# Third cycle of the rotations: the couplings of two blocks in one product of two columns, and the last pair turned and added between the products of its second layer

## The chip, the cores and the metric

The kernel runs on one core of a Trainium2 chip. The metric is the device time of one execution in microseconds, given as the median of several runs. The engines are TensorE (PE in the profile, with PEld for its weight loads), VectorE (DVE), ScalarE (ACT), GpSimd (POOL) and SyncE (SP), which here only issues DMAs.

## The reference

A small hybrid network on `x` of 2 x 2048 tokens x 256 features, all in fp32. Two attentions alternate with two uses of the same feed-forward part:

```python
x = x + attn_a(layernorm(x))
x = x + ffn(layernorm(x))
x = x + attn_b(layernorm(x))
x = x + ffn(layernorm(x))

def ffn(x):
    gf = global_net(x.mean(axis=1))                # one value a batch
    out = x
    for _ in range(3):                             # three cycles
        h = gelu(out @ w1 + b1)                    # 256 -> 256
        h = gelu(h @ w2 + b2)                      # 256 -> 128
        h = gelu(h @ w3 + b3)                      # 128 -> 64
        tf = sigmoid(h @ w4 + b4)                  # 64 -> 1, one value a token
        coupling = 0.1 + adaptive_range * (0.7 * gf + 0.3 * tf - 0.5) * 2.0
        o_r, o_i, p_r, p_i = split(out, 4)
        out = out + coupling * concat(p_r, -p_i, -o_r, o_i)
    return out
```

The change is in the third cycle of `ffn` and in the addition of its result to `x`.

## The kernel before

**Tiling.** The 4096 tokens are cut into 8 blocks of 512 (`BLK`). The normalized input of a feed-forward part lies feature-major in `zq` (128 partitions x 2 halves of the features x 4096 tokens), the residual stream `x` token-major in `xs` (128 tokens x 32 tiles x 256 features). All of this stays in on-chip memory; `x` is written out by the last feed-forward part.

**The rotations.** `rotations(n, part, store)` makes the steps of feed-forward part n (0 between the attentions, 1 at the end, where `store` is true). A step k = 0 to 11 stands for one pair of blocks, 2 * (k % 4) and the next, in cycle k // 4; so k = 8 to 11 are the third cycle. For each k:

- `first(k, e)` (L789) takes block e of the pair through w1: two halves m of the 256 outputs, each a product (L796) into its own PSUM bank and a Gelu on ACT (L797).
- `second(k)` (L800): w2 for both blocks, L806, Gelu L808.
- `third(k)` (L811): w3 for both blocks (L816). The 64 outputs of block 0 stand in rows 0 to 63 of one bank, those of block 1 in rows 64 to 127, so that one Gelu (L818) makes one tile `a3` of 128 rows for the pair.
- `fourth(k)` (L821): the couplings, and the block turned. In the first two cycles the coupling is made for all rows at once and `z` is changed in place (L829 to L841). In the third cycle it goes to `back` (L843).

**`back`.** The result of the third cycle is wanted token-major, to be added to `xs`. So the couplings are made by token: for each block e of the pair, four products (L851), one for each 128 tokens, of 64 rows of `a3` and the column `w4`, each giving 128 tokens x 1. In fp32 each product shows as two records in the profile, so 16 for a pair. Then a tanh of 128 x 4 on ACT (L856), the coupling from it on DVE (L857) and its negative (L858). After both blocks' couplings come the halves: for each block e and each half h of its tokens, TensorE turns 2 x 2 squares of `z` into one bank `trf` (L870), DVE adds it to `xs` in two operations of 128 x 256 (L874), then adds the twisted quarters times the coupling in four operations of 128 x 128 (L882, `scalar_tensor_tensor`), and, in the second feed-forward part, SP issues a DMA of 256 KB (L888) that stores the half.

**The order.** The program order on each engine is the one in which the steps are called; nothing reorders it afterwards. In the steady part `rounds(f, n)` (L1173) calls for even n `fourth(k - 2)`, `second(k - 1)`, `first(k, 0)` and for odd n `third(k - 1)`, `first(k, 1)`, with k = n // 2. The end of the first feed-forward part is written out by hand, with the steps of attention b's first blocks, `zero` and `one`, between:

```python
        zero.norm(work)
        first(11, 0)
        third(10)
        one.look()
        first(11, 1)
        one.norm(late)
        fourth(10)
        second(11)
        zero.turn()
        third(11)
```

after which come `zero.query()`, `zero.rotate()`, `zero.key()` and `fourth(11, zero.rotate)` (the latter calls a second `rotate` between the two blocks of the pair). The second feed-forward part ends with `for n in range(8, 27): rounds(f, n)`: its last calls are `fourth(9)`, `second(10)`, `first(11, 0)`, `third(10)`, `first(11, 1)`, `fourth(10)`, `second(11)`, `third(11)`, `fourth(11)`.

**Buffers.** `bank()` gives the next of seven PSUM banks in turn, so an operation of TensorE that opens a bank waits until the one that had it seven banks ago has been read. `take("small", ...)` gives the next of eight buffers in a ring, `hold.tile` a place for good.

**Names in the profile.** `q1f`, `q2f`, `q3f`, `q4f` are the banks of the four layers, `trf` those of the transposes; `a1f`, `a2f`, `a3f` the Gelus' results; `cf` the couplings. `pv`, `rotk`, `swapks` belong to attention b; `p1f` and `gmf` to the global net (`context`, L767), `L945` to attention b's projections.

Of the kernel before, what the change touches and what calls it, by code (L numbers as in the profile page):

```python
# [9 lines left out]
F32 = mybir.dt.float32  # L10
F32R = mybir.dt.float32r
AF = mybir.ActivationFunctionType
ALU = mybir.AluOpType
# [3 lines left out]
P = 128  # L17
B, N, D = 2, 2048, 256
# [3 lines left out]
BPB = N // BLK  # L22
# [45 lines left out]
def tile_hybrid(ctx: ExitStack, tc: tile.TileContext, x: bass.AP, consts: bass.AP, wa_d: bass.AP, wf_d: bass.AP, wb_d: bass.AP, out: bass.AP):  # L68
    nc = tc.nc
    mm = nc.tensor.matmul  # L70

    keep = ctx.enter_context(tc.tile_pool(name="keep", bufs=1))
    small = keep.tile([P, _CONST["cols"][0]], F32, name="small")
# [4 lines left out]
    zq = keep.tile([P, 2, T], F32, name="zq")  # L78
# [6 lines left out]
    def const(name):  # L85
        return small[:, _CONST[name][0] : _CONST[name][1]]

    def view(t, at, name, rows=P):
        return t[:rows, at[name][0] : at[name][1]]

    ident, mean_w, ones = const("ident"), const("mean"), const("ones")
    sign = const("sign")

    def blk(t, j):
        return t[:, :, j * BLK : (j + 1) * BLK]

    def tokens(j):
        return xs[:, 4 * j : 4 * j + 4, :]
# [37 lines left out]
    def in_order(first, which=(engines.PE, engines.DVE, engines.Activation, engines.Pool)):  # L136

        last = {}
        for ins in nc.cur_bb.bb.instructions[first:]:
            if ins.engine in which:  # L140
                if ins.engine in last:
                    tc.add_manual_dep(
                        ins, last[ins.engine].name,
                        mybir.DependencyInfo(mybir.DependencyClass.NoSync, mybir.DependencyReason.DATA),
                        reason="order of the program",
                    )
                last[ins.engine] = ins
# [563 lines left out]
    def behind(tail):  # L711
        wf, wb = weights["wf"], weights["wb"]
        late = later_pools["late"]
        hold = ctx.enter_context(tc.tile_pool(name="hold", bufs=1, reuse_waits="tile"))
# [8 lines left out]
        def take(tag, shape, name):  # L723
            if tag == "kt2":
                return work.tile(shape, F32, tag="kt", name=name)
            if tag in ("og", "kt", "swap"):
                return own.tile(shape, F32, tag=tag, name=name, bufs=2 if tag == "swap" else 1)
            return work.tile(shape, F32, tag=tag, name=name, bufs=rings.get(tag, 1))

        def bank(name):  # L730
            return ps.tile([P, BLK], F32, tag="ps", name=name)
# [6 lines left out]
        w4, b3 = view(wf, _WF, "w4"), view(wf, _WF, "b3")  # L738
# [5 lines left out]
        hb4 = hold.tile([P, 1], F32, name="f_hb4")  # L744
# [4 lines left out]
        plain = hold.tile([P, 1], F32, name="f_plain")  # L749
        nc.vector.tensor_scalar(plain, view(wf, _WF, "range"), 0.3, None, ALU.mult)  # L750
        beta = hold.tile([P, 1], F32, name="f_beta")
        nc.vector.tensor_scalar(beta, plain, sign, None, ALU.mult)

        def rotations(n, part, store):
            alphas, plains = {}, {}
            acts, narrow = {}, {}

            def context(b):

# [26 lines left out]
            def blocks(k):  # L786
                return 2 * (k % 4), 2 * (k % 4) + 1

            def first(k, e):  # L789

                z = blk(zq, blocks(k)[e])
                a1 = take((("qs", "ks"), ("rotq", "rotk"))[k % 2][e], [P, 2, BLK], f"a1f{n}_{k}_{e}")
                for m in range(2):
                    q1 = bank(f"q1f{n}_{k}_{e}_{m}")
                    for c in range(2):
                        mm(q1, w1[:, c, m * P : (m + 1) * P], z[:, c, :], start=(c == 0), stop=(c == 1))  # L796
                    nc.scalar.activation(a1[:, m, :], q1, AF.Gelu, bias=b1[:, m : m + 1])  # L797
                acts[k, e] = a1

            def second(k):  # L800
                narrow[k] = []
                for e in range(2):
                    a1 = acts.pop((k, e))
                    q2 = bank(f"q2f{n}_{k}_{e}")
                    for c in range(2):
                        mm(q2, w2[:, c, :], a1[:, c, :], start=(c == 0), stop=(c == 1))  # L806
                    a2 = take("en", [P, BLK], f"a2f{n}_{k}_{e}")
                    nc.scalar.activation(a2, q2, AF.Gelu, bias=b2)  # L808
                    narrow[k].append(a2)

            def third(k):  # L811

# [8 lines left out]
            def fourth(k, between=None):  # L821
# [8 lines left out]
                for e in range(2):  # L830
# [9 lines left out]
                    nc.vector.tensor_tensor(z[:, 0, :], z[:, 0, :], t0, ALU.add)  # L840
                    nc.gpsimd.tensor_tensor(z[:, 1, :], z[:, 1, :], t1, ALU.subtract)  # L841

            def back(k, js, a3, between):  # L843


                both = []
                for e in range(2):
                    row = slice(64 * e, 64 * e + 64)
                    q4 = bank(f"q4f{n}_{k}_{e}")
                    for tile in range(4):  # L850
                        mm(  # L851
                            q4[:, tile : tile + 1], a3[row, tile * P : (tile + 1) * P], w4[row, 0:1],
                            start=True, stop=True,
                        )
                    tt = take("small", [P, 3, 4], f"cf{n}_{k}_{e}")
                    nc.scalar.activation(tt[:, 2, :], q4[:, 0:4], AF.Tanh, bias=hb4, scale=0.5)  # L856
                    nc.vector.tensor_scalar(tt[:, 0, :], tt[:, 2, :], plain, plains[js[e] // BPB], ALU.mult, ALU.add)  # L857
                    nc.vector.tensor_scalar(tt[:, 1, :], tt[:, 0, :], -1.0, None, ALU.mult)  # L858
                    both.append(tt)
                for e in range(2):  # L860
                    j, cs, z = js[e], both[e], blk(zq, js[e])
                    if e == 1 and between:
                        between()
                    for h in range(2):
                        tr = bank(f"trf{n}_{k}_{e}_{h}")
                        for q in range(2):
                            at = slice((2 * h + q) * P, (2 * h + q + 1) * P)
                            for c in range(2):
                                to = q * D + (1 - c) * P
                                nc.tensor.transpose(tr[:, to : to + P], z[:, c, at], ident)  # L870
                        tr = tr.rearrange("p (q s f) -> p q s f", q=2, s=2)
                        half = tokens(j)[:, 2 * h : 2 * h + 2, :].rearrange("p q (s f) -> p q s f", s=2)
                        for s in range(2):
                            nc.vector.tensor_tensor(half[:, :, s, :], half[:, :, s, :], tr[:, :, 1 - s, :], ALU.add)  # L874
                        for q in range(2):
                            tile = 2 * h + q

                            x4, t4 = (
                                a.rearrange("p s (u f) -> p (s u) f", u=2) for a in (half[:, q, :, :], tr[:, q, :, :])
                            )  # L880
                            for m, quarters in enumerate((slice(0, 4, 3), slice(1, 3))):
                                nc.vector.scalar_tensor_tensor(  # L882
                                    x4[:, quarters, :], t4[:, quarters, :], cs[:, m, tile : tile + 1],
                                    x4[:, quarters, :], ALU.mult, ALU.add,
                                )
                        if store:
                            s0 = (j % BPB) * BLK + 2 * h * P
                            nc.sync.dma_start(  # L888
                                out[j // BPB, s0 : s0 + 2 * P, :].rearrange("(t p) d -> p t d", p=P),
                                tokens(j)[:, 2 * h : 2 * h + 2, :],  # L890
                            )

            return context, first, second, third, fourth


        sums1 = hold.tile([P, 2, NB], F32, name="sums1")
# [273 lines left out]
        blocks = [Block(j) for j in range(NB)]  # L1170
        tail = tail(bank)

        def rounds(f, n):  # L1173

            context, first, second, third, fourth = f
            k = n // 2
            if n % 2 == 0:
                if 0 <= k - 2:
                    fourth(k - 2)
                if 0 <= k - 1 < 12:  # L1180
                    second(k - 1)
                if k < 12:
                    first(k, 0)
            else:
                if 0 <= k - 1:
                    third(k - 1)
                if k < 12:
                    first(k, 1)

        f = rotations(0, sums0, False)  # L1190
        context, first, second, third, fourth = f
        turned, looked = first_norms, {}

        def block_of(j):
# [91 lines left out]
        one.turn()  # L1286

        f = rotations(1, sums1, True)
        context, first, second, third, fourth = f
        front, front1 = context(0), context(1)  # L1290
        for j, x in enumerate(blocks):
            before = blocks[j - 1] if j else None
# [76 lines left out]
        third(2)  # L1369
        first(3, 1)  # L1370
        next(front1)
        for n in range(8, 27):
            rounds(f, n)
        in_order(begin)

    behind(attention_a())
# [117 lines left out]
```

## Time and profile before

| | us |
|---|---|
| median of 3 runs | 2184.47 (2184.06 to 2188.18) |
| the profiled execution | 2182.7 |
| its span | 2180.8 |
| TensorE busy in it | 2136.0 |
| mean granted TensorE clock | 0.993 |
| one step k of the second feed-forward part in its steady rounds | 14.86 |
| last scaled add (L882) ends | 2177.73 |

Times of single events are counted from the start of the span. The clock is given as a share of full speed. Attention a takes the first 1,560 us or so; the third cycle of the first feed-forward part begins about 1696 and runs into attention b at 1733 to 1757; the second feed-forward part's third cycle ends with the program. In a row of a timeline, the columns are start, duration, engine, line, operation, result and operands, shape and count; in the chain of waits, start and duration of a piece of work that the end waited for.

### The profile page before, as it was taken

To read this page: it belongs to the slowest core of one execution; us is meant where nothing else is said; L and a number is where in the kernel's file an instruction comes from. 1 tells how busy PE (TensorE), PEld (TensorE's weight loads), DVE (VectorE), ACT (ScalarE), POOL (GpSimd) and SP (SyncE) were. 2 spreads that over 40 slices of the span, in tenths; PEclk is the share of its full clock that TensorE was granted. 3 is DMA by queue.
4 is the path that set the end of the run, shared out by engine and by line. 5 is a ranking of instruction groups with operands and counts; after the bars stand their busy time and mean duration, and the time that the engine had idled before them with its cause. 6 is when DMAs were issued, how large, how long until landed. Compare 5 with 4: busy or idle time off the path is not lost.

```text
span 2180.8 us, 38972 instructions
## 1 busy us (share of the span) xinstructions
PE 2136.0 (98%) x14346; PEld 1028.5 (47%) x14346; DVE 1725.7 (79%) x3319; ACT 1434.0 (66%) x2780; POOL 348.6 (16%) x318
## 2 busy tenths in 40 slices
PE   8899999999999999999999999999999999999998
PEld 3344444444444444444444444444444567676434
DVE  6789998998999899899899899987144688886435
ACT  3367777777776777777677777777864445554442
POOL 3100000000001000000000000000145345541450
PEclk9999999999999999999999999999999999999999
DMA  6410110101101011010110101100100000000002
GB/s 184 135 58 14 41 36 16 46 12 45 36 16 45 10 48 36 16 39 17 48 35 17 36 19 48 36 16 7 51 1 1 1 1 2 1 2 1 1 0 78
DMA packets 53552, 68.21 MB, mean 31 GB/s; under 512 B 18800, under 2 KB 27888, under 8 KB 53104
## 3 DMA queue, kind: packets, MB, share of 16 engines
q1 hardware_dynamic: 52448, 64.26, 10.6%
q8 instruction: 113, 1.85, 0.3%
q10 hardware_dynamic: 720, 0.92, 0.1%
q14 instruction: 79, 0.65, 0.1%
q0 software_dynamic: 192, 0.52, 0.1%
HBM read 35.26 MB, written 25.69 MB: 28 GB/s over the span
## 4 chain that ended last, share of the span: by engine, by line
PE 86%; DVE 8%; DMA 2%; ACT 1%; SPq 1%; issue 1%; POOL 1%; DVEq 0%; ACTq 0%; POOLq 0%
PE av L620 21%; PE s L378 19%; PE p L633 10%; PE q1f L796 7%; PE p L637 7%; DVE mx L382 5%; PE q2f L806 4%; PE pe L1084 2%; PE po L487 2%; PE bpo L1110 1%; PE pv L954 1%; PE pw L954 1%; PE pq L945 1%; PE q3f L816 1%; PE pk L945 1%; DMA xs<-in_x 1%
## 5 line engine op out<-in xcount | busy, mean ns | idle before, releaser
L382 DVE TENSOR_REDUCE mx<-s 128x1 f32<-128x512 f32 x2048 | 1272.9, 683 | 118.1 <-PE s L378 116.4
L641 ACT ACTIVATE e<-p 128x512 f32<-128x512 f32 x2048 | 1060.7, 605 | 356.9 <-PE p L637 353.3
L378 PE MATMUL s<-a_kP,qP 64*128 64x512 f32 x2048 | 706.7, 470 | 19.5 <-DVE mx L382 17.4
L637 PE MATMUL p<-a_m,a_pick 64*128 64x512 f32 x2048 | 589.5, 416 | 0.0
L378 PEld LDWEIGHTS s<-a_kP,qP 64*128 64x128 f32 x2048 | 283.1, 184 | 578.9 <-DVE mx L382 549.8
L620 PE MATMUL av<-e,a_v 128*32 128x512 f32 x4096 | 550.2, 605 | 0.0
L633 PE MATMUL p<-qP,a_kP 64*128 64x512 f32 x2048 | 529.1, 394 | 2.3 <-ACT e L641 2.3
L633 PEld LDWEIGHTS p<-qP,a_kP 64*128 64x128 f32 x2048 | 286.4, 185 | 62.8 <-ACT e L641 26.9
L637 PEld LDWEIGHTS p<-a_m,a_pick 64*128 64x128 f32 x2048 | 283.9, 184 | 29.4
L481 POOL TENSOR_TENSOR oc<-oc,sums 128x512 f32<-128x512 f32 x16 | 20.8, 1299 | 1232.7 <-DMA sums<-dr 907.1
L796 PE MATMUL q1f<-zq,wf 128*128 128x512 f32 x384 | 175.5, 600 | 0.0
L620 PEld LDWEIGHTS av<-e,a_v 128*32 128x32 f32 x4096 | 81.4, 108 | 128.5 <-issue 119.8
L797 ACT ACTIVATE a1f<-q1f,wf 128x512 f32<-128x512 f32 x96 | 66.0, 688 | 99.6 <-PE q1f L796 96.2
L796 PEld LDWEIGHTS q1f<-zq,wf 128*128 128x128 f32 x384 | 70.6, 190 | 98.0 <-issue 86.3
L806 PE MATMUL q2f<-a1f,wf 128*128 128x512 f32 x192 | 89.6, 610 | 0.0
L1090 DVE TENSOR_TENSOR en<-pe,small 128x512 f32<-128x512 f32 x128 | 79.4, 683 | 12.7 <-PE pe L1084 12.6
L835 DVE TENSOR_SCALAR cf<-cf,f_beta,alphaf 128x512 f32<-128x512 f32 x32 | 33.6, 1050 | 53.7 <-ACT cf L834 53.6
L839 POOL TENSOR_TENSOR tf<-cf,zq 128x512 f32<-128x512 f32 x32 | 55.6, 1737 | 92.0 <-DVE cf L835 91.7
L808 ACT ACTIVATE a2f<-q2f,wf 128x512 f32<-128x512 f32 x48 | 32.7, 687 | 54.9 <-PE q2f L806 54.9
L841 POOL TENSOR_TENSOR zq<-zq,tf 128x512 f32<-128x512 f32 x32 | 56.8, 1775 | 3.1 <-DVE tf L838 0.7
L806 PEld LDWEIGHTS q2f<-a1f,wf 128*128 128x128 f32 x192 | 35.2, 193 | 45.3 <-issue 44.4
L840 DVE TENSOR_TENSOR zq<-zq,tf 128x512 f32<-128x512 f32 x32 | 22.2, 693 | 36.2 <-POOL tf L839 36.0
(207 smaller groups left out, 1674.0 us busy)
## 6 DMA issues: line engine op xcount, KB each, us to landing
qP<-dq SPq DMA_DIRECT2D x64, 256.0 KB
dq<-qh SPq DMA_DIRECT2D x62, 128.0 KB
dq<-ql SPq DMA_DIRECT2D x62, 128.0 KB
a_kP<-dk SPq DMA_DIRECT2D x16, 256.0 KB
oc<-avs SPq DMA_DIRECT2D x128, 32.0 KB
sums<-dr SPq DMA_DIRECT2D x128, 32.0 KB
out<-xs SPq DMA_DIRECT2D x16, 256.0 KB
xs<-in_x SPq DMA_DIRECT2D x7, 512.0 KB
```

Source lines behind the costliest of these rows:

```text
L378: mm(s, qP[r // 2][row, qi * P : (qi + 1) * P], kP[r // 2][row, k0 + kb * BLK : k0 + (kb + 1) * BLK], start=True, stop=True,)
L382: nc.vector.tensor_reduce(mx[:, qi, r : r + 1, kb], s, AX.X, ALU.max)
L620: mm(av[32 * r : 32 * r + 32, :], vA[:, units[u][0] // BPB * KB + kb, 32 * r : 32 * r + 32], es[r], start=(kb == 0), stop=(kb == KB - 1),)
L633: mm(t[r], kP[r // 2][row, k0 : k0 + P], qP[r // 2][row, :], start=True, stop=False)
L637: mm(t[r], pick[row, :], mrow[r // 2][row, :], start=False, stop=True)
L641: nc.scalar.activation(es[r], t[r], AF.Exp, scale=1.0 / HD**0.5)
L796: mm(q1, w1[:, c, m * P : (m + 1) * P], z[:, c, :], start=(c == 0), stop=(c == 1))
L797: nc.scalar.activation(a1[:, m, :], q1, AF.Gelu, bias=b1[:, m : m + 1])
L806: mm(q2, w2[:, c, :], a1[:, c, :], start=(c == 0), stop=(c == 1))
L839: nc.gpsimd.tensor_tensor(t1, cs, z[:, 0, :], ALU.mult)
L841: nc.gpsimd.tensor_tensor(z[:, 1, :], z[:, 1, :], t1, ALU.subtract)
L1090: nc.vector.tensor_tensor(self.ens[t][w], pes[w].rearrange("p (h n) -> p h n", h=4), const("triu").unsqueeze(1).to_broadcast([P, 4, P]), A ...
```

## The change

It has two parts.

1. **One product for two blocks** (k = 8 to 11 of both feed-forward parts). A constant `w4_pair` of 128 x 2 holds `w4` in rows 0 to 63 of column 0 and in rows 64 to 127 of column 1, and zeros elsewhere. Four products of all 128 rows of `a3` with it give the couplings of both blocks side by side, in one bank. One tanh, one L857 and one L858, each of 128 x 8, take the place of two of each of 128 x 4. The tile is made on GpSimd, by one memset and two copies, ahead of attention b's constants.
2. **The last pair of the program** (k = 11 of the second feed-forward part). The transposes and adds of a half become a function of their own, `turn_back`. The last calls are written out: `fourth(10)` between the two halves of `first(11, 1)`; in `second(11)` behind each block's product and Gelu the transposes and adds of that block (`turn_ahead`); `third(11)`; and `fourth(11)`, which then has the couplings, the scaled adds and the stores left.

```diff
+        w4_pair = hold.tile([P, 2], F32, name="f_w4_pair")
+        nc.gpsimd.memset(w4_pair, 0.0)
+        for e in range(2):
+            row = slice(64 * e, 64 * e + 64)
+            nc.gpsimd.tensor_copy(w4_pair[row, e : e + 1], w4[row, 0:1])
...
-            def first(k, e):
+            def first(k, e, between=None):
...
                 for m in range(2):
+                    if m == 1 and between:
+                        between()
...
-            def second(k):
+            def second(k, behind=None):
...
                     narrow[k].append(a2)
+                    if behind:
+                        behind(e)
...
+            def turn_back(k, e, h):
+                j = blocks(k)[e]
+                z = blk(zq, j)
+                tr = bank(f"trf{n}_{k}_{e}_{h}")
+                for q in range(2):
+                    at = slice((2 * h + q) * P, (2 * h + q + 1) * P)
+                    for c in range(2):
+                        to = q * D + (1 - c) * P
+                        nc.tensor.transpose(tr[:, to : to + P], z[:, c, at], ident)
...
+                for s in range(2):
+                    nc.vector.tensor_tensor(half[:, :, s, :], half[:, :, s, :], tr[:, :, 1 - s, :], ALU.add)
+                return half, tr
+
+            def turn_ahead(k, e):
+                for h in range(2):
+                    turned[k, e, h] = turn_back(k, e, h)
...
-                both = []
+                q4 = bank(f"q4f{n}_{k}")
+                for tile in range(4):
+                    mm(
+                        q4[:, 2 * tile : 2 * tile + 2], a3[:, tile * P : (tile + 1) * P], w4_pair,
+                        start=True, stop=True,
+                    )
+                cs = take("small", [P, 3, 8], f"cf{n}_{k}")
+                nc.scalar.activation(cs[:, 2, :], q4[:, 0:8], AF.Tanh, bias=hb4, scale=0.5)
+                nc.vector.tensor_scalar(cs[:, 0, :], cs[:, 2, :], plain, plains[js[0] // BPB], ALU.mult, ALU.add)
+                nc.vector.tensor_scalar(cs[:, 1, :], cs[:, 0, :], -1.0, None, ALU.mult)
                 for e in range(2):
-                    row = slice(64 * e, 64 * e + 64)
-                    q4 = bank(f"q4f{n}_{k}_{e}")
-                    for tile in range(4):
-                        mm(
-                            q4[:, tile : tile + 1], a3[row, tile * P : (tile + 1) * P], w4[row, 0:1],
-                            start=True, stop=True,
-                        )
-                    tt = take("small", [P, 3, 4], f"cf{n}_{k}_{e}")
-                    nc.scalar.activation(tt[:, 2, :], q4[:, 0:4], AF.Tanh, bias=hb4, scale=0.5)
-                    nc.vector.tensor_scalar(tt[:, 0, :], tt[:, 2, :], plain, plains[js[e] // BPB], ALU.mult, ALU.add)
-                    nc.vector.tensor_scalar(tt[:, 1, :], tt[:, 0, :], -1.0, None, ALU.mult)
-                    both.append(tt)
...
+                        half, tr = turned.pop((k, e, h), None) or turn_back(k, e, h)
...
-                                    x4[:, quarters, :], t4[:, quarters, :], cs[:, m, tile : tile + 1],
+                                    x4[:, quarters, :], t4[:, quarters, :], cs[:, m, 2 * tile + e : 2 * tile + e + 1],
...
-        for n in range(8, 27):
+        for n in range(8, 23):
             rounds(f, n)
+        third(10)
+        first(11, 1, lambda: fourth(10))
+        second(11, lambda e: turn_ahead(11, e))
+        third(11)
+        fourth(11)
```

On the engines: TensorE has 8 records of the couplings a k where it had 16; ACT 8 tanh less in all, DVE 16 small operations less; GpSimd three operations more in the setup. At the end TensorE's order is third layer of k = 10, half of `first(11, 1)`, couplings and transposes of k = 10, the other half, w2 of one block, its transposes, w2 of the other, its transposes, third layer and couplings of k = 11; DVE's is couplings and four halves of k = 10, the eight adds of k = 11, its two small operations, its 16 scaled adds. SP's order of stores is the same.

More of the change, by code (lines that the diff above doesn't have):

```diff
@@ L752, in behind @@
         nc.vector.tensor_scalar(beta, plain, sign, None, ALU.mult)
+        w4_pair = hold.tile([P, 2], F32, name="f_w4_pair")
[3 more added lines that the diff above has]
+            nc.gpsimd.tensor_copy(w4_pair[row, e : e + 1], w4[row, 0:1])
         def rotations(n, part, store):
             alphas, plains = {}, {}
-            acts, narrow = {}, {}
+            acts, narrow, turned = {}, {}, {}
             def context(b):
@@ L841, in fourth @@
                     nc.gpsimd.tensor_tensor(z[:, 1, :], z[:, 1, :], t1, ALU.subtract)
-            def back(k, js, a3, between):
-                both = []
-                for e in range(2):
-                    row = slice(64 * e, 64 * e + 64)
-                    q4 = bank(f"q4f{n}_{k}_{e}")
-                    for tile in range(4):
-                        mm(
-                            q4[:, tile : tile + 1], a3[row, tile * P : (tile + 1) * P], w4[row, 0:1],
-                            start=True, stop=True,
-                        )
-                    tt = take("small", [P, 3, 4], f"cf{n}_{k}_{e}")
-                    nc.scalar.activation(tt[:, 2, :], q4[:, 0:4], AF.Tanh, bias=hb4, scale=0.5)
-                    nc.vector.tensor_scalar(tt[:, 0, :], tt[:, 2, :], plain, plains[js[e] // BPB], ALU.mult, ALU.add)
-                    nc.vector.tensor_scalar(tt[:, 1, :], tt[:, 0, :], -1.0, None, ALU.mult)
-                    both.append(tt)
-                for e in range(2):
-                    j, cs, z = js[e], both[e], blk(zq, js[e])
+            def turn_back(k, e, h):
[7 more added lines that the diff above has]
+                        nc.tensor.transpose(tr[:, to : to + P], z[:, c, at], ident)
+                tr = tr.rearrange("p (q s f) -> p q s f", q=2, s=2)
+                half = tokens(j)[:, 2 * h : 2 * h + 2, :].rearrange("p q (s f) -> p q s f", s=2)
+                for s in range(2):
+                    nc.vector.tensor_tensor(half[:, :, s, :], half[:, :, s, :], tr[:, :, 1 - s, :], ALU.add)
+                return half, tr
@@ new lines, in turn_ahead @@
+            def turn_ahead(k, e):
+                for h in range(2):
+                    turned[k, e, h] = turn_back(k, e, h)
+            def back(k, js, a3, between):
+                q4 = bank(f"q4f{n}_{k}")
[8 more added lines that the diff above has]
+                nc.vector.tensor_scalar(cs[:, 1, :], cs[:, 0, :], -1.0, None, ALU.mult)
+                for e in range(2):
+                    j = js[e]
@@ L864, in back @@
                     for h in range(2):
[L865 to L874, printed above, removed]
+                        half, tr = turned.pop((k, e, h), None) or turn_back(k, e, h)
                         for q in range(2):
@@ L891, in back @@
                             )
-            return context, first, second, third, fourth
+            return context, first, second, third, fourth, turn_ahead
         sums1 = hold.tile([P, 2, NB], F32, name="sums1")
@@ L1173, in rounds @@
         def rounds(f, n):
-            context, first, second, third, fourth = f
+            context, first, second, third, fourth, _ = f
             k = n // 2
@@ L1190, in behind @@
         f = rotations(0, sums0, False)
-        context, first, second, third, fourth = f
+        context, first, second, third, fourth, _ = f
         turned, looked = first_norms, {}
@@ L1288, in behind @@
         f = rotations(1, sums1, True)
-        context, first, second, third, fourth = f
+        context, first, second, third, fourth, turn_ahead = f
         front, front1 = context(0), context(1)
```

## The prediction

> **What bounds the kernel now.** I began with the page's totals and with the engines of the chain that ended last:
>
> ```profile
> PE 2136.0 (98%) x14346; PEld 1028.5 (47%) x14346; DVE 1725.7 (79%) x3319; ACT 1434.0 (66%) x2780; POOL 348.6 (16%) x318
> ...
> PE 86%; DVE 8%; DMA 2%; ACT 1%; SPq 1%; issue 1%; POOL 1%; DVEq 0%; ACTq 0%; POOLq 0%
> ```
>
> TensorE works 98% of the span. The change touches only k = 8 to 11 of each feed-forward part, so I then cut the trace into stretches (columns: length, then busy time of PE, PEld, DVE, ACT and POOL, granted clock, DMA share, GB/s):
>
> ```profile
> 1690.00:1735.00 45.00, 45.00 (x190) 23.52 (x188) 27.02 (x97) 20.64 (x37) 11.55 (x14) 1.00 0.00 1
> 1735.00:1760.00 25.00, 21.81 (x115) 14.16 (x116) 22.17 (x54) 11.79 (x23) 10.39 (x8) 0.93 0.00 1
> ...
> 2055.00:2145.00 90.00, 90.00 (x261) 37.24 (x259) 35.63 (x63) 40.86 (x62) 42.37 (x24) 1.00 0.04 12
> 2145.00:2181.00 36.00, 25.73 (x122) 14.55 (x122) 24.11 (x84) 8.26 (x16) 0.00 (x0) 0.92 0.26 89
> ```
>
> The reader is to see two regimes. In 1690 to 1735 (k = 8 and after, first FFN) and 2055 to 2145 (second FFN) TensorE is never idle: what it no longer executes shortens the program one for one. In the other two rows, where k = 11 meets attention b and where the program ends, it idles: 3.2 and 10.3 us, and the next view is who ends last. The chain of waits of the end (start, duration):
>
> ```profile
> 2158.62 1.45 PE q4f L851 x16
> 2160.07 1.90 PE trf L870 x16
> 2161.97 3.44 PE q2f L806 x8
> 2165.40 1.93 PE q3f L816 x4
> ...
> 2167.35 0.70 ACT a3f L818
> ...
> 2168.09 1.06 PE q4f L851 x11
> ...
> 2169.18 0.28 ACT cf L856
> ...
> 2169.48 0.30 DVE cf L857
> ...
> 2170.45 0.66 DVE xs L874 x2
> ...
> 2171.14 1.13 DVE xs L882 x4
> ```
>
> The last pair's 16 products, tanh, four small DVE operations and then four halves of adds and scaled adds run in series. The halves start at 2170.36, 2172.18, 2174.00 and 2175.82; the last ends at 2177.73, and the span 3.07 us later, the last store's issue and flight.
>
> **The products of the couplings.** Sixteen products of 64 rows and one column per k become eight of 128 rows and two columns. The sixteen fill 1.45 us (first row of the fence). Nothing at 128 rows and two columns is in the trace; the nearest is the context's product (L767), full height and one column:
>
> ```profile
> 2038.08 0.52 PEld L767 LDWEIGHTS p1f<-gmf,wf 128*128 128x128 f32 x4 [2.82 <-DVE gmf L763]
> ```
>
> That is 0.52 us for four loads of 0.19 each, so they start (0.52 − 0.19)/3 = 0.11 apart; eight take 0.88. One column against two is nothing beside the load of 128 columns. The saving is **0.57 a k**. Here a rule speaks against the change. The Trainium skill, "TensorE: Matmul & The Clock Gate", section "LDWEIGHTS (loading the stationary operand)", has the load depend on columns alone, about 107 ns for 128; so 16 × 0.107 = 1.71 would become 0.85, a saving of 0.86. But its section "The mechanism" (packing small matmuls) says that a load runs ahead of products under way when they hold other row groups, and full-height tiles give that up. The row shows it: sixteen half-height loads take 1.45, not 1.71. I take the rows' 0.57; ends 0 (full-height tiles twice as dear) and 0.86.
>
> **First FFN, start of attention b.** For k = 8 and 9 the saving counts fully: 1.14. For k = 10 I take 0.3 of 0.57, since its coupling operations on DVE are already stretched to 0.54 and 0.65 us beside a GpSimd operation (L987, 1727.56 to 1730.35) and its halves are near the edge. For k = 11 TensorE is not the limit, DVE is:
>
> ```profile
> 1746.08 0.91 DVE L857 TENSOR_SCALAR cf<-cf,f_plain,plainf 128x4 f32<-128x4 f32 x1
> 1746.92 1.27 POOL L1004 TENSOR_TENSOR rotk<-ks,rope 128x512 f32<-128x512 f32 x1
> 1747.03 1.19 DVE L858 TENSOR_SCALAR cf<-cf 128x4 f32<-128x4 f32 x1
> ...
> 1748.13 1.31 DVE L857 TENSOR_SCALAR cf<-cf,f_plain,plainf 128x4 f32<-128x4 f32 x1
> 1748.14 1.27 POOL L1006 TENSOR_TENSOR swapks<-swapks,rope 128x512 f32<-128x512 f32 x1
> ```
>
> Each of DVE's small operations, 0.17 to 0.30 us elsewhere, ends only as a GpSimd operation does. The second pair (1748.13 to the first half's start at 1749.55, 1.42 us) is gone; the halves follow, TensorE waits for them (2.58 us idle before 1751.51). I take 1.3, against the ends of 0 (the GpSimd operation of 1748.14 stretches the first adds in their stead) and 1.42. Sum for the first FFN: 1.14 + 0.3 + 1.3 = **2.74**. From there to 2143 the program is bound by TensorE or by its chain with DVE, and is moved bodily.
>
> **The clock there.** TensorE's granted clock is 0.57, 0.50, 0.50 in the three microseconds from 1752, after those 2.58 us of idle; eight products of pv take 3.19 us where the same eight took 1.99 at 1745.88. The change shortens the gap to some 2.0. The same page, section "What's actually happening", gives half rate after an idle window of some 3.4 us: then neither gap should throttle, and 0 is gained; by the row, 2.58 sufficed, and if 2.0 does not, up to some 1.2 us of pv come back, of which I estimate 0.6 to 0.8 is not hidden by DVE. I take 0, with 0.8 in the range.
>
> **Second FFN.** k = 8 and 9 save 1.14, so the third layer of k = 10, at 2153.98 in the chain, starts 2152.84 on the old clock (the 2.74 left aside). Then TensorE in its new order: third layer 1.01; half of the pair's w1 product 1.82 (of 3.63); the couplings of k = 10 0.88; its transposes 1.90; the other half 1.82; w2 of one block 1.72 (of 3.44), its eight transposes 0.95, w2 of the other 1.72, its transposes 0.95; third layer 1.01. Sum 13.78: it ends at 2166.62 where it ended at 2167.33. The 0.9 that the third layer waited for the Gelu of a2 (1.93 against 1.01) is covered by the transposes between, 0.95 against 0.76 for the Gelu (0.70 and a handover): close, and worth at most 0.2 if it misses.
>
> Of what the move makes wait: the tanh of k = 10 stands on ACT ahead of the second half's Gelu, but its products lie 3.7 us before that half ends. The transposes of k = 11 need four of seven banks, which come free when k = 10's tanh, its first two halves on DVE and the Gelu of a2 are done; I find 2.6 to 3.4 us of room. Behind them on TensorE stand w2 and the last third layer. On DVE the k = 10 halves run from some 2157.5 to 2164.8 (4 × 1.82), then eight adds of about 0.35 to 2167.7, before the couplings are there; their stores are moved with k = 10, about 1 us earlier, and SP holds nothing else.
>
> Then: Gelu a3 +0.76 → 2167.38; products and tanh: 1.09 before with eight loads 0.083 apart, now 1.2 → 2168.58; L857 +0.30 → 2168.88; L858 +0.33 → 2169.21; first scaled add +0.08 → 2169.29. Before, four small operations took 2169.48 to 2170.36; one pair is gone. Sixteen scaled adds follow with no adds between: four take 1.13, one 0.344, so they start 0.26 apart: 15 × 0.26 + 0.344 = 4.24 → **2173.53**, against 2177.73. Stores then come every 1.04 us; a 256 KB store moves in 0.75 to 1.0, so none queues for more than a trifle and the tail stays 3.07. This part gives **4.20** (1.14 of it from k = 8 and 9). The move itself is about even up to the couplings; the gain lies in 4 × 0.74 of adds gone from DVE's tail.
>
> **At nothing:** the setup of the new tile (three small GpSimd operations at about 1560, with some 8 us to their next user; ends 0 and 0.6), eight tanh less on ACT (not the limit in these rounds).
>
> **Sum.** 2.74 + 4.20 = 6.94 off the profiled execution: its time 2182.7 (span 2180.8 and 1.9 around it) becomes 2175.8. The median shown is 2184.47, 1.8 above that execution; with the same difference **2177.5 us**. No change is within 0.2%, 4.4 us, about what a measurement can tell: 2180.1 to 2188.8.
>
> **Rivals.**
> - *More is gained* (0.10): the clock's half rate at 1752 goes too, loads follow the rule of columns: 2.1 more, about 2175.4. For it, the short gap; against, a clock of 0.50 also appears at 2039 after 2.7 us, so the threshold is not far from either gap.
> - *GpSimd goes on holding DVE* at 1748 (0.15): the first adds are stretched as the small pair was, and 1.3 stays: 2178.8. For it, each of four DVE rows ends with a GpSimd row; against, L874 and L882 show no such stretch in the end, but no GpSimd runs there.
> - *Full-height products are twice as dear* (0.07): 1.45 remains per k. Lost are 1.44 in the first FFN, 1.14 in k = 8, 9 and 1.14 in the last two: 3.7, so 2181.2, no change. Against it: the context's row.
> - *The turning ahead doesn't get ahead* (0.05): a bank comes free late and the eight adds (2.9 us) still stand between couplings and end: 2180.4, at the edge of no change. Against it: room of 2.6 us or more.
> - *Slower* (0.05): the tile of two columns is placed before attention b's constants and work buffers and moves their addresses by 32 bytes. If engines then read or write some of them more slowly, it acts on the 620 us from 1560 to the end, and it decides from 1.15% (6.94 / 620); at 2%, 12.4 us more, less 6.9: 2190. Against it: products on tiles at either offset last the same here, 592 ns in L945 and in L796.
>
> **Numbers.** The forecast has 0.58, its own range 2175.8 to 2179. The range of 2173.8 to 2181.0 takes in the first two rivals and the turning ahead, leaving part of the fourth and the slower one out. Faster 0.83: forecast, first two rivals; within 0.2%: 0.12; slower 0.05.
>
> **What would show it.** In the profile after: eight records of the coupling products in about 0.9 us; 16 scaled adds 0.26 apart at the end with no add among them; third layer of k = 11 with no wait; the halves at attention b's start some 2.7 us earlier; from there to 2143 no change in length. The forecast is wrong if the first adds there are stretched, if the eight adds end after the last couplings, or if the stretch from 1760 to 2000 changes by more than 1 us.

## The result, and the profile after

| | before | after |
|---|---|---|
| median, us | 2184.47 (5 runs, 2183.82 to 2188.28) | 2176.65 (5 runs, 2174.11 to 2177.89) |
| profiled execution, us | 2182.7 | 2177.89 |
| its span, us | 2180.8 | 2176.1 |

The ratio of the times is 0.9956, 95% interval 0.9942 to 0.9971: 0.44% faster, 7.8 us. The profiled execution is only 4.7 us shorter in span, so it must be cut into stretches before anything is read from it. The marks are the starts of events that both traces have:

| from ... to the next mark | before | after | forecast | measured |
|---|---|---|---|---|
| start of the span: first Gelu of the first feed-forward part | 1565.51 | 1567.25 | 0 | +1.74 |
| to the first coupling product of k = 8 | 130.97 | 130.88 | 0 | -0.09 |
| to the couplings of k = 11 on DVE | 49.60 | 47.63 | -1.44 | -1.97 |
| to the first half of k = 11 | 3.47 | 2.03 | -1.30 | -1.44 |
| to the first pe of attention b | 7.99 | 8.05 | 0 | +0.06 |
| to the global net's product p1f, second part | 280.54 | 280.49 | 0 | -0.05 |
| to the first w1 product of k = 3 | 5.68 | 7.36 | 0 | +1.68 |
| to the third layer of k = 10 | 110.15 | 108.63 | -1.14 | -1.52 |
| to the end of the last scaled add | 23.82 | 20.33 | -3.06 | -3.49 |
| to the end of the span | 3.07 | 3.45 | 0 | +0.38 |

The four changed rows give 8.4 us. Two rows that lie outside the changed steps, +1.74 and +1.68, hide 3.4 of it in this one execution; without them the span is 8.1 shorter, beside the medians' 7.8. A second profile of the changed kernel, further down, shows both rows to vary between executions of the same program.

The stretches of the trace after, with columns as before (length, busy time of PE, PEld, DVE, ACT and POOL, clock, DMA share, GB/s):

```profile
1735.00:1760.00 25.00, 22.19 (x111) 14.13 (x110) 22.17 (x54) 11.47 (x23) 10.73 (x9) 0.93 0.00 1
2055.00:2145.00 90.00, 90.00 (x258) 37.87 (x257) 36.02 (x65) 40.56 (x61) 42.31 (x24) 1.00 0.04 12
```

TensorE is still full in the second feed-forward part and still idles where attention b begins. The end, in the chain of waits of the trace after:

```profile
2155.32 0.79 PE q4f L878 x8
2156.11 1.80 PE trf L862 x16
2157.91 1.72 PE q1f L804 x4
2159.63 1.72 PE q2f L814 x4
2161.34 0.87 PE trf L862 x8
2162.22 1.72 PE q2f L814 x4
2163.94 0.87 PE trf L862 x8
2164.81 1.06 PE q3f L826 x4
...
2166.63 1.07 PE q4f L878 x8
```

Each piece begins where the one ahead ends: no bank is waited for, and the last third layer takes 1.06 where it took 1.93 with its wait. The eight records of the couplings take 0.79, not 1.45. DVE meanwhile (its timeline in the trace after):

```profile
2163.09 1.13 DVE L899 SCALAR_TENSOR_TENSOR xs<-trf,cf,xs 128x128 f32<-128x128 f32 x4
2164.14 2.73 DVE L866 TENSOR_TENSOR xs<-xs,trf 128x256 f32<-128x256 f32 x8
2168.03 0.29 DVE L884 TENSOR_SCALAR cf<-cf,f_plain,plainf 128x8 f32<-128x8 f32 x1 [1.17 <-ACT cf L883]
```

The eight adds of the last pair are done at 2166.87 and DVE waits 1.17 us for the last tanh. After it only the 16 scaled adds remain, 4.22 us from 2168.43 to 2172.65.

### The profile page after: what moved, and what is told of

Read it like the earlier page. It is cut to its first block, busy times and chain, and to the rows that moved or that the text cites. A ratio compares the mean times of both kernels' runs of the same rounds, so it can differ in the third digit from the quotient of the medians.

```text
span 2176.1 us, 38825 instructions
## 1 busy us (share of the span) xinstructions
PE 2133.1 (98%) x14282; PEld 1025.1 (47%) x14282; DVE 1719.8 (79%) x3303; ACT 1429.3 (66%) x2772; POOL 349.0 (16%) x321
## 4 chain that ended last, share of the span: by engine, by line
PE 87%; DVE 8%; DMA 2%; ACT 1%; SPq 1%; issue 1%; POOL 1%; ACTq 0%; DVEq 0%; POOLq 0%
PE av L620 21%; PE s L378 20%; PE p L633 10%; PE q1f L804 8%; PE p L637 6%; DVE mx L382 5%; PE q2f L814 4%; PE pe L1101 2%; PE po L487 2%; PE bpo L1127 1%; PE pq L962 1%; PE pv L971 1%; PE pw L971 1%; PE pk L962 1%; PE q3f L826 1%; PE b_sums L1143 1%
## 5 line engine op out<-in xcount | busy, mean ns | idle before, releaser
L633 PE MATMUL p<-qP,a_kP 64*128 64x512 f32 x2048 | 528.6, 394 | 2.2 <-ACT e L641 2.2
L633 PEld LDWEIGHTS p<-qP,a_kP 64*128 64x128 f32 x2048 | 286.8, 186 | 64.3 <-ACT e L641 26.8
L1107 DVE TENSOR_TENSOR en<-pe,small 128x512 f32<-128x512 f32 x128 | 79.4, 683 | 12.8 <-PE pe L1101 12.7
```

The source lines that it names most:

```text
L633: mm(t[r], kP[r // 2][row, k0 : k0 + P], qP[r // 2][row, :], start=True, stop=False)
L1107: nc.vector.tensor_tensor(self.ens[t][w], pes[w].rearrange("p (h n) -> p h n", h=4), const("triu").unsqueeze(1).to_broadcast([P, 4, P]), A ...
```

## The experiments

Between executions of one kernel the time varies by as much as 8 or 9 us (27 runs of the kernel before, beside the first four experiments: 2182.5 to 2190.4; 14 of one variant: 2174.4 to 2183.5). In the ten profiles taken the first Gelu of the first feed-forward part comes between 1565.51 and 1573.65, though ahead of it the kernels differ in no more than the few small setup operations on GpSimd and DVE. Stretches behind it, where two kernels have the same steps, agree within 0.1 us but for the two places where TensorE's clock drops. So the experiments are judged by stretches of their profiles, and by ratios with the kernel before on the same chip.

### One product for two blocks, alone

```diff
-        for n in range(8, 23):
-            rounds(f, n)
-        third(10)
-        first(11, 1, lambda: fourth(10))
-        second(11, lambda e: turn_ahead(11, e))
-        third(11)
-        fourth(11)
+        for n in range(8, 27):
+            rounds(f, n)
```

> The one product for two blocks alone; the end of the program is called as before. Theory (the two parts add up, and each product saved is saved from the path): from the first coupling product of k = 8 in the first feed-forward part to the first pe of attention b it is shorter than before by 3.4 us, as in the changed kernel; k = 8 and 9 of the second part 1.5 us shorter; from the third layer of k = 10 to the last scaled add 23.75 becomes 22.5 (0.75 in k = 10, 0.5 for one pair of DVE operations less). Some 2178.5 us in all. Rival (the gain at attention b comes from the ring of small buffers or from chance, not from the products and the pair of operations): the stretch up to pe differs from the changed kernel's by over 0.5 us.

Ratio 0.9971 (0.9958 to 0.9983). From the coupling product of k = 8 to pe it takes 57.71 us, as in the changed kernel to the hundredth (61.06 before); the stretch with k = 8 and 9 of the second part 108.64 (108.63; 110.15); third layer of k = 10 to the last scaled add 22.60, against 23.82. The theory held. Its chain of waits shows what the part alone leaves in place:

```profile
2158.05 3.44 PE q2f L814 x8
2161.49 1.93 PE q3f L826 x4
...
2165.57 0.30 DVE cf L884
...
2166.06 0.67 DVE xs L866 x2
```

The third layer waits for its Gelu again (1.93), and adds follow the couplings.

### The turning ahead, alone

The changed kernel with the couplings of before in `back`, for each block:

```diff
-                q4 = bank(f"q4f{n}_{k}")
...
+                for e in range(2):
+                    row = slice(64 * e, 64 * e + 64)
+                    q4 = bank(f"q4f{n}_{k}_{e}")
+                    for tile in range(4):
+                        mm(q4[:, tile : tile + 1], a3[row, tile * P : (tile + 1) * P], w4[row, 0:1], start=True, stop=True)
```

with its own tanh and two DVE operations.

> The turning ahead alone; the couplings as before, 16 products of 64 rows and two pairs of DVE operations. Theory: nothing changes up to the third layer of k = 10 of the second part; from there to the last scaled add 23.75 becomes 21.5, since the adds (4 x 0.74 = 3.0) leave DVE's tail and the move of work behind the w1 half costs some 0.7 on TensorE. Some 2182.2 us in all. Rival (the two parts need each other: with two banks and two tanh more per k, a bank comes free late and TensorE waits before the transposes or the last third layer): 22.5 or more, with a wait of TensorE at trf or q3f between the w2 products.

Third layer of k = 10 to the last scaled add: 21.54. All stretches ahead are those of before within 0.1. Ratio 0.9993 (0.9984 to 1.0001): by times alone it couldn't be told from no change, by its stretch it gains 2.28. No bank is waited for in its chain either:

```profile
2161.28 1.45 PE q4f L875 x16
2162.73 1.90 PE trf L856 x16
...
2168.94 1.72 PE q2f L808 x4
2170.66 0.87 PE trf L856 x8
2171.53 1.06 PE q3f L820 x4
```

The two parts add up: 23.82 - 22.60 = 1.22 and 23.82 - 21.54 = 2.28 make 3.50, and together they gave 3.49.

### The height of the products, by itself

```diff
-                    mm(
-                        q4[:, 2 * tile : 2 * tile + 2], a3[:, tile * P : (tile + 1) * P], w4_pair,
-                        start=True, stop=True,
-                    )
+                    for e in range(2):
+                        mm(
+                            q4[:, 2 * tile + e : 2 * tile + e + 1], a3[:, tile * P : (tile + 1) * P], w4_pair[:, e : e + 1],
+                            start=True, stop=True,
+                        )
```

> The changed kernel with each of the four products of a pair made twice, one column at a time, so that there are again 16 records, but of all 128 rows. Theory (loads of different row groups overlap in part, loads of full height don't): 16 take 1.58 us (twice the 0.79 of the changed kernel) to 1.75, over the 1.45 of 16 of 64 rows. Rival (a load costs by its columns alone, whatever its rows, and half-height tiles gain nothing): 1.45, as before.

In its chain of waits, k = 10 (one execution, so only the stretches are read):

```profile
2161.43 1.68 PE q4f L879 x16
2163.11 1.81 PE trf L862 x16
```

Sixteen of full height take 1.68, twice the eight's 0.79 and a little more, and over the 1.45 of sixteen of half height: the theory held. How the half-height loads overlap can be seen by counting those that run in equal stretches of 0.45 us, in the middle of the sixteen (length, busy time of PEld and its loads, clock, DMA share, GB/s), first in the trace of before, then in this kernel's:

```profile
2158.99:2159.44 0.45, 0.45 (x9) 1.00 0.00 0
2174.08:2174.53 0.45, 0.45 (x6) 1.00 0.00 0
```

The loads' starts show it in full. Full-height loads start 0.11 us apart throughout. Of the half-height ones the first four start 0.11 apart, the next eight in pairs with 0.03 between the two and a pair every 0.11, the last four 0.11 apart again. The first tanh, which waits for block 0's eight records, could start after eleven of the sixteen (in the prediction's chain of waits), so a pair is one load of each block: half the loads of the one run beside half of the other's, and within a block a half-height load costs the same 0.11 as a full one.

Full height has a gain of its own at both ends. The loads of k = 10 in the traces of before (two rows) and after:

```profile
2158.55 1.44 PEld L851 LDWEIGHTS q4f<-wf,a3f 64*128 64x128 f32 x16 [0.76 <-issue]
2160.00 1.73 PEld L870 LDWEIGHTS trf<-small,zq 128*128 128x128 f32 x16
...
2154.73 0.19 PEld L878 LDWEIGHTS q4f<-f_w_pair,a3f 128*128 128x128 f32 x1 [0.24 <-issue]
2155.86 1.82 PEld L862 LDWEIGHTS trf<-small,zq 128*128 128x128 f32 x16
```

Before, the first load of the couplings and that of the transposes start together with the first of their products, at 2158.55 and 2160.00. After, they start 0.43 and 0.11 us ahead of them (2155.16 and 2155.97), while the products before them still run. So eight loads take seven intervals (0.79) and sixteen of full height fifteen (1.68), and the transposes behind full-height products take 1.80 or 1.81, where behind 64-row products they take 1.90, before and with the turning ahead alone.

### The place of k = 10

```diff
-        first(11, 1, lambda: fourth(10))
+        first(11, 1)
+        fourth(10)
```

> The changed kernel with the couplings and transposes of k = 10 behind both halves of the pair's w1 product instead of between them. Theory (DVE has 1.2 us of room before the last couplings): DVE starts k = 10 by 1.72 us later, the eight adds end some 0.6 us behind the last tanh, and from the third layer of k = 10 to the last scaled add 20.26 becomes 20.9. Rival (the banks decide): TensorE waits for banks of k = 10 at the transposes of k = 11 or at the last third layer, and it becomes 22 or more. Third case: no difference, and the place of k = 10 was worth nothing.

20.80 us, 0.47 over the changed kernel; ratio to before 0.9969 (0.9961 to 0.9977). Its DVE timeline:

```profile
2170.75 2.73 DVE L866 TENSOR_TENSOR xs<-xs,trf 128x256 f32<-128x256 f32 x8
2173.39 0.29 DVE L884 TENSOR_SCALAR cf<-cf,f_plain,plainf 128x8 f32<-128x8 f32 x1
```

No idle time stands ahead of L884 any more: the adds have become what is late, by the 1.72 us of the moved half less DVE's 1.17 of room, 0.55 worked out. So the place between the halves buys the room, and all but 0.5 us of the gain is there without it.

### Why the small operations took 2 us at attention b's start

The changed kernel still shows this in DVE's timeline:

```profile
1745.76 0.89 DVE L884 TENSOR_SCALAR cf<-cf,f_plain,plainf 128x8 f32<-128x8 f32 x1
1746.68 1.20 DVE L885 TENSOR_SCALAR cf<-cf 128x8 f32<-128x8 f32 x1
1747.79 0.74 DVE L866 TENSOR_TENSOR xs<-xs,trf 128x256 f32<-128x256 f32 x2
```

and in GpSimd's:

```profile
1745.35 1.27 POOL L1023 TENSOR_TENSOR swapks<-swapks,rope 128x512 f32<-128x512 f32 x1 [1.35 <-DVE swapks L1022]
1746.58 1.26 POOL L1021 TENSOR_TENSOR rotk<-ks,rope 128x512 f32<-128x512 f32 x1
1747.81 1.25 POOL L1023 TENSOR_TENSOR swapks<-swapks,rope 128x512 f32<-128x512 f32 x1
```

The two small operations end as a GpSimd operation does, but the adds beside the third (1747.79) take their usual 0.74. The adds have one operand in PSUM; the small ones go from SBUF to SBUF. The Trainium skill, "SBUF — State Buffer", section "Who interferes with whom", says just this: DVE's copies and `tensor_scalar` between SBUF tiles can enter a mode that takes the port pair shared with GpSimd, and the later of the two then blocks for the other's whole instruction, while a DVE instruction with at most one SBUF input outside that mode doesn't. The edit moves the tile to PSUM and leaves engine, count and order alone; the second operation also no longer reads the first one's result. That alone would not help: at k = 8 of the changed kernel, with no GpSimd operation beside, the pair takes 0.40 us to the first add with both in SBUF (1699.42 to 1699.82).

```diff
-                nc.scalar.activation(cs[:, 2, :], q4[:, 0:8], AF.Tanh, bias=hb4, scale=0.5)
-                nc.vector.tensor_scalar(cs[:, 0, :], cs[:, 2, :], plain, plains[js[0] // BPB], ALU.mult, ALU.add)
-                nc.vector.tensor_scalar(cs[:, 1, :], cs[:, 0, :], -1.0, None, ALU.mult)
+                nc.scalar.activation(q4[:, 8:16], q4[:, 0:8], AF.Tanh, bias=hb4, scale=0.5)
+                nc.vector.tensor_scalar(cs[:, 0, :], q4[:, 8:16], plain, plains[js[0] // BPB], ALU.mult, ALU.add)
+                nc.vector.tensor_scalar(cs[:, 1, :], q4[:, 8:16], minus, plains[js[0] // BPB], ALU.mult, ALU.subtract)
```

> The changed kernel with the tanh of the couplings written to free columns of its PSUM bank, and both small DVE operations reading it there (the second as -plain times tanh minus the other constant, from a constant made in the setup), so that neither reads on-chip SBUF but for the per-row constants. Theory (a DVE operation from SBUF to SBUF waits for a running GpSimd operation, one with its tile in PSUM doesn't): at the start of attention b the two take 0.4 us to the first half instead of 2.03, TensorE's wait before pv shrinks from 2.1 by as much, its half clock there goes, and the stretch from the first coupling product of k = 8 to the first pe becomes 57.7 - 1.6 = 56.1, or down to 55.5 with the clock. Rival (GpSimd's operation holds any small DVE operation, or what ends there is something that GpSimd and DVE both wait for): 2.0 and 57.7 as now.

GpSimd's and DVE's timelines of this kernel:

```profile
1747.57 1.28 POOL L1026 TENSOR_TENSOR swapks<-swapks,rope 128x512 f32<-128x512 f32 x1 [1.35 <-DVE swapks L1025]
1747.96 0.27 DVE L887 TENSOR_SCALAR cf<-q4f,f_plain,plainf 128x8 f32<-128x8 f32 x1
1748.15 0.27 DVE L888 TENSOR_SCALAR cf<-q4f,f_minus,plainf 128x8 f32<-128x8 f32 x1
1748.34 0.74 DVE L869 TENSOR_TENSOR xs<-xs,trf 128x256 f32<-128x256 f32 x2
```

0.38 us to the first half where it was 2.03, in the middle of a GpSimd operation: the theory held. TensorE's wait before pv falls from 2.10 to 0.26 us, and the stretch from k = 8 to pe from 57.71 to 55.29: 1.65 by the small operations, 0.55 since pv here has the full clock (7.50 from the first half to pe, not 8.05), 0.22 ahead of them, in k = 10, whose pair also ran beside a GpSimd operation. Ratio to before 0.9955 (0.9941 to 0.9968), which the times alone could not tell from the changed kernel's.

### The half clock before k = 3

The row of +1.68 in the table needed an explanation of its own. TensorE waits there twice, for a3 and for the mean of the second batch. In the trace of before:

```profile
2034.96 1.13 PE L829 MATMUL q4f<-a3f,wf 64*128 64x512 f32 x4 [0.79 <-ACT a3f L818]
2038.08 0.61 PE L767 MATMUL p1f<-gmf,wf 128*128 128x1 f32 x4 [1.99 <-DVE gmf L763]
```

The changed kernel has the same two waits, 0.79 and 1.97 us. After them TensorE is granted half its clock. In the changed kernel's first profile that lasts (stretches of one microsecond, the clock third from the end):

```profile
2036.00:2037.00 1.00, 0.67 (x4) 0.67 (x4) 0.97 (x3) 0.00 (x0) 0.45 (x2) 0.71 0.00 0
2037.00:2038.00 1.00, 1.00 (x3) 0.63 (x3) 0.45 (x1) 0.26 (x1) 1.00 (x1) 0.50 0.00 0
...
2043.00:2044.00 1.00, 1.00 (x3) 0.38 (x2) 0.28 (x1) 0.11 (x1) 1.00 (x1) 0.88 0.00 0
```

Counting a share s of clock lost as 2s of the microsecond at half rate, with 0.50 in all six between, that is 0.58 + 6 + 0.24 = 6.8 us. In the trace of before the five microseconds from 2038 have 0.94, three times 0.50, and 0.86: 3.4 us. To see whether the waiting causes it, `second(2)` was given to TensorE to do meanwhile:

```diff
         third(1)
         next(front1)
+        second(2)
         fourth(1)
         next(front1)
-        second(2)
         first(3, 0)
```

> The changed kernel with second(2) of the second feed-forward part called ahead of fourth(1) and of the global net's first product, so that TensorE has the w2 products to do while it waits for a3 (0.8 us) and for the mean gmf (2.0 us). Theory (TensorE's half clock after that wait comes from the idle time, and its length, 3.3 us in most profiles and 6.5 us in the changed kernel's first one, is chance): no microsecond there with a clock under 1.00, and the stretch from the first pe of attention b to the first w1 product of k = 3 becomes 281.5 where it was 286.2 in most profiles and 287.9 in one. Rival (the half clock comes at a time or from the load of the other engines): it stays, and only the 2.8 us of waits go, 283.4; or DVE or GpSimd is what is late, and it stays at 286.

TensorE's timeline of this kernel:

```profile
2034.80 3.70 PE L814 MATMUL q2f<-a1f,wf 128*128 128x512 f32 x8
2038.43 1.13 PE L839 MATMUL q4f<-a3f,wf 64*128 64x512 f32 x4
2039.49 0.61 PE L773 MATMUL p1f<-gmf,wf 128*128 128x1 f32 x4
```

No wait and no microsecond under 1.00 at this place; from pe to the first w1 product of k = 3 it takes 281.70 where it took 286.2 to 287.9. Ratio 0.9941 (0.9929 to 0.9954). Of the 4.5 us gained on the usual case 2.8 are the two waits and 1.7 the clock (3.4 us at half rate). The two were taken away together, so which of them the half clock needs was not tried.

That the length was chance needed the changed kernel once more.

> The changed kernel once more, for a second profile of it. Theory (the longer half clock before k = 3 of the second feed-forward part is chance): from the global net's first product to the first w1 product of k = 3 it takes 5.68 us, as in the profiles of before and of four variants, and not 7.36; all other stretches agree with its first profile within 0.1 us, and from the first Gelu of the first feed-forward part to the end it takes 607.2. Rival (the length goes with something in this very program): 7.36 again and 608.9.

5.67 us at this place, and 606.6 from the first Gelu to the end, against 608.85 in its first profile; ratio 0.9961 (0.9949 to 0.9974). One thing was expected wrong: the first half of k = 11 to pe took 7.48, not 8.05. TensorE's rows for pv, first profile and second:

```profile
1749.74 3.64 PE L971 MATMUL pv<-wb,bz 128*128 128x256 f32 x8 [2.10 <-DVE xs L899]
```

```profile
1752.10 1.99 PE L971 MATMUL pv<-wb,bz 128*128 128x256 f32 x8 [2.11 <-DVE xs L899]
```

The same program with the same wait, once at half and once at full clock: this too is chance from one execution to the next. The other profiles agree: of the five with a wait of 2.10 to 2.12 us here, four have pv at 2.62 to 3.64 us and one at 1.99; the two with 2.56 and 2.58 have 2.93 and 3.19; the three with 1.01 (the sixteen full-height products) and 0.26 (twice) have 1.99.

### Both edits on the changed kernel

> The two edits together on the changed kernel. Theory: both stretches as alone, so from the first Gelu of the first feed-forward part to the end of the span 607.2 - 1.6 - 4.7 = 600.9, up to 0.6 less, against 615.3 before. Rival (an earlier start of attention b is lost again, since its blocks are paced by DVE or GpSimd): 602.5.

600.36 us from the first Gelu to the end (615.29 before; 606.6 and 608.85 in the changed kernel's two profiles). Median 2171.83 us against 2186.36 of the kernel before beside it, ratio 0.9932 (0.9919 to 0.9944): faster than before by 0.68%, and its interval hardly meets the changed kernel's first one (0.9942 to 0.9971). The gains of the two edits add up, and attention b hands the earlier start on whole: its stretch from pe to p1f takes 281.22, as with the second edit alone (281.23).

## Why the prediction was right

- **The sum.** 2177.5 was forecast and 2176.65 measured; 6.94 us less and 7.82. It is right by its own steps, not by errors that cancel: each changed stretch moved the way it was said to, each by some more (together 8.42). That the medians come within 0.9 us of the forecast is in part luck: the interval of the ratio leaves 6.3 to 12.7 us.
- **The products.** The saving per k was taken as 0.57 and is 0.75, the term that was mis-sized everywhere: 0.66 in the products and 0.09 in the transposes behind them, of which nothing had been thought. The interval of 0.11 read from the nearest row is right; what was left out is that the first load runs ahead under the w1 product, so that eight take seven intervals, 0.79 and not 0.88, and that the transposes gain the same way. The rule of columns would have said 0.86. What spoke against the change, that loads of different row halves overlap, is true between the two blocks and worth 1.68 - 1.45 = 0.23 us in sixteen records; half as many records outweigh it. But full height doesn't give up running ahead of products under way, as the prediction had it: the row at 2154.73 shows one that does.
- **k = 10 of the first part.** 0.3 was taken. Two steps at 0.75 leave 1.97 - 1.50 = 0.47 for it.
- **The pair of small operations.** 1.3 was taken, 1.44 came. The rival that GpSimd would stretch the first adds instead is refuted, and for a reason that the first trace already allowed: an operand in PSUM. It should not have had 0.15.
- **The clock at attention b's start.** Taken as no gain, with up to 0.8 open. It is a matter of chance at a wait of 2.1 us and worth 0.57 (8.05 against 7.48). The 2.7 us that the prediction puts ahead of the half clock at 2039 are two waits, 0.79 and 1.99, with products between.
- **The end.** TensorE's 13.78 from the third layer of k = 10 are 13.48 (2152.39 to 2165.87): three tenths from couplings and transposes. The a2 wait is covered as said (1.06 for the third layer), the banks have room, the adds end 1.17 us ahead of the couplings where about 1 was said, and 16 scaled adds take 4.22 (4.24). That the gain lies in the adds leaving DVE's tail is shown by the turning ahead alone.
- **The tail of the last store**, taken as unchanged, is 3.45 instead of 3.07. It is 3.37 to 3.45 in all eight profiles with the turning ahead and 3.07 and 3.15 in the two without it (the spans are read to 0.1 us), so it goes with the turning ahead, after which the last stores follow each other more closely; how it comes about was not tried.
- **The rival of addresses** (which would decide from 6.94 / 620 = 1.12%, not 1.15) is refuted for this shift: from pe to p1f, 280 us on the moved tiles, 280.54 became 280.49, and without the new tile (the turning ahead alone) it is 280.49 too.

## What to carry to other kernels

Where one engine is full, count the records of its small operations: merging eight half-height products into four full-height ones halves the loads and saves nearly half of their time (1.45 to 0.79 us); loads in a row start 0.11 us apart at either height, and what is lost is the overlap of loads in different row halves. At the end of a program move whatever doesn't need the last result ahead of it, under the other engine's work, and check that its engine has room there; here the place of one step decided between 1.2 us of room and half a microsecond of delay. A small DVE operation that takes as long as the GpSimd operation beside it can be freed by having its tile in PSUM, as the pair here that went from 2.03 us to 0.38.

## What was not expected of the hardware

- Waits of TensorE of about 2 us were enough for half clock: in all eight profiles that have one of 1.96 to 1.99 us ahead of the global net's product (with 0.79 us of waiting shortly before it), and in four of five that have one of 2.10 to 2.12 ahead of pv. The Trainium skill, "TensorE: Matmul & The Clock Gate", section "What's actually happening", speaks of an idle window of about 3.4 us that runs freely; the free running fits the chance and the two lengths seen, 3.4 and 6.8 us (one window and two), but the idle time needed here was less.
- Between 1565.5 and 1573.7 us pass up to the first Gelu of the first feed-forward part, from execution to execution, and 1567.25 and 1569.60 in the two profiles of the very same program, so that single times of this kernel differ more than the change does. Of these 8.1 us, 5.6 are there by the first product of L633 in attention a, which starts between 100.88 and 106.49 us. What varies there was not tried.
